# A fused convolution, scan and expert kernel: the cross-half exponents of the scan taken from rows spread by DMA and a bias of the exponential

## The chip, the core and the metric

The kernel runs on one core of one Trainium2 chip. The metric is device time in microseconds (us) of one execution, as the median of several runs. A profile is one further execution, taken by the hardware profiler, with its own time. The engines are named as the profile names them: PE does matmuls (PEld is its weight load), DVE is the vector engine, ACT the scalar engine with the activation tables, POOL the general engine, and SP issues every DMA of this kernel in one queue, in order.

## The reference, cut to what matters

The input is 128 images of 128 channels and 16 x 16 pixels, so 256 tokens per image. Layer 0 is a group norm and two quantised 3 x 3 convolutions with batch norm. Layer 1 is a state-space scan in both directions (`fwd` and `bwd`), added to the tokens, and a mixture of 8 experts of which each token takes 2. The change lies in the scan. For one direction (4 heads `h`, head width 64, state width 64) it is:

```
dt = softplus(dt + dt_bias);  A = -exp(A_log)
dA = dt * A;  xdt = xh * dt
Acs = cumsum(dA) within a chunk of 64 tokens
Y_diag = sum over s<=l of  C[l].B[s] * exp(Acs[l] - Acs[s]) * xdt[s]
states = sum over s of     B[s] * exp(Acs[last] - Acs[s]) * xdt[s]
carry  = states + carry * exp(Acs[last])          # chunk after chunk
Y_off  = C[l] . carry * exp(Acs[l])
y = (Y_diag + Y_off + xh * D) * silu(z);  RMS norm;  out_proj
```

Chunking is only a way to compute it: over the whole image, y[l] is the sum over all earlier s of C[l].B[s] * exp(cum[l] - cum[s]) * dt[s] * xh[s], with cum the running sum of dA over the 256 tokens.

## The kernel before

**The early stages.** The first 300 us or so load the images, do both convolutions and write the transposed tokens to DRAM (`y_d`). What follows is one long recorded stretch over 64 tiles `i` of two images (512 tokens) each.

**How the scan is done.** An image is cut into two halves of 128 tokens. For a tile `i`, a direction `d` and an image `k` of the tile there are three blocks of 128 source tokens (on the partitions) by 128 target tokens, for each of the 4 heads: first half to first half, first half to second half (the block between the halves), second to second. "First" is half `d`, so it is turned round for the backward direction. The exponents of one block are made by PE as one bank `sg` of 128 x 512 (4 heads x 128 targets) in `part_s`, ACT takes the exponential into `e` (tile `e0` holds the two blocks with the first half as source, `e1` the third), DVE multiplies by C.B (`g_ps`) in `part_m` (L929, L934), and PE multiplies by the tokens in `part_y` (L948, L954), which is the last reader of `e0` and `e1`. `e0` and `e1` have 4 buffers each.

**Where the exponents come from.** `part_c` works once for a group of 4 images, that is, for a pair of tiles. From dt it makes `daz` (dA) and `lwz` (minus the log of dt), and PE forms in bank `r_ps` (L784, L787, L788) three strips of 128: the running sums, the negated remaining sums with `lwz`, and `lwz` alone. DVE splits them into three bf16 parts (`part` and `left`, L794 and L797), since the exponents are rebuilt by bf16 matmuls; the parts go to DRAM (`parts_d`, L802) and come back to `rows` and `cols` (L810, L815) in the layout that `part_s` multiplies. `part_s` has three steps `j`: the two blocks within a half (two matmuls of 256 columns, L913, with a mask of -1e30 in `cols`) and the block between the halves (one matmul of 512 columns, L915).

**What sets the order.** Each `part_*` function is a stream of steps that yields between them. A table `T` written out by hand gives each step of each part its place, once for the even and once for the odd tile of a pair, and `PERIOD` is the shift from one pair to the next; all steps are sorted by place and recorded in that order. Each place is used once in a period, so that 372 places are 372 steps. Every engine works off its instructions in recorded order, and waits are put in by the framework: a buffer's next writer waits for its last reader. So a step's place fixes what stands ahead of it on its engine and, for a DMA, in SP's queue.

**Banks.** PSUM has eight banks in three groups: "x" (2) for `x_ps`, `z_ps` and `sg`, "y" (2) for `y_ps` and `f_ps`, "o" (4) for the rest. A bank of "x" comes free when ACT (for `z_ps` and `sg`) or ACT and DVE (for `x_ps`, L836 and L842) have read it.

**Other names in the text.** `part_p` loads the gates of two experts, spread over the partitions, into `gb` (L1109) and POOL multiplies the tokens into it (L1113); `part_f` multiplies by the experts (L1125) and frees `gb`. `part_o` is the output projection (L1008). `act` is the helper for all activations that need a table (its instructions stand at L675).

Of the kernel before, what the change touches and what calls it, by code (L numbers as in the profile page):

```python
# [8 lines left out]
F32 = mybir.dt.float32  # L9
# [5 lines left out]
P = 128  # L15
# [19 lines left out]
def kernel(ctx: ExitStack, tc: tile.TileContext, a: dict):  # L35
# [20 lines left out]
    parts_d = [dram.tile([2, 3, G * NH * 4, 3, P], BF16, name=f"parts_{i}", tag=f"parts_{i}") for i in range(2)]  # L56
# [558 lines left out]
    cols = [late.tile([P, 2, 2, 2, 3, P], BF16, name=f"cols{k}") for k in range(3)]  # L615
    far = late.tile([HD, 1], BF16, name="far")

    def constants():
        nc.gpsimd.memset(far, -1e30)
        none = sm.tile([NR, 3, 3 * P], BF16, name="none", tag="part", bufs=1)  # L620
        nc.gpsimd.memset(none[:, :, :P], 0.0)
        for k in range(2):
            nc.sync.dma_start(parts_d[k][1, :, :, 2, :].rearrange("q r l -> r q l"), none[:, :, :P])
        for k in range(3):
            r, c = rows[k], cols[k]
            nc.scalar.copy(r.rearrange("p h d t l -> p h (d t l)"), heads.unsqueeze(2).to_broadcast([P, NH, 4 * P]))
            nc.vector.tensor_copy(
                r[0:HD].rearrange("p h d t (f l) -> p (h d t f) l", l=HD),
                ident[0:HD, 0:HD].unsqueeze(1).to_broadcast([HD, 2 * NH * 2 * 2, HD]),
            )  # L630
            nc.vector.tensor_copy(
                c.rearrange("p m d j f l -> p m (d j f l)"), triple.unsqueeze(2).to_broadcast([P, 2, 12 * P])
            )
            for d in range(2):
                for half in range(2):
                    sign = 1 - 2 * d
                    for m in range(2):
                        nc.gpsimd.affine_select(
                            out=c[0:HD, m, d, :, half, :], in_=far.unsqueeze(2).to_broadcast([HD, 2, P]),
                            pattern=[[0, 2], [sign, P]], compare_op=ALU.is_ge, fill=0.0,  # L640
                            base=-sign * HD * half - 1, channel_multiplier=-sign,
                        )
# [10 lines left out]
    BANKS = {"x": 2, "y": 2, "o": 4}  # L653

# [11 lines left out]
    yts, uTs, xcs, xts, bcs, ccs, zs = {}, {}, {}, {}, {}, {}, {}  # L666
    table = ["none"]

    def act(out, in_, func):
# [5 lines left out]
        nc.scalar.activation(out, in_, func)  # L675
# [40 lines left out]
    def part_c(g):  # L716
# [66 lines left out]
        for d in range(2):  # L783
            nc.tensor.matmul(  # L784
                r_ps[:, : 2 * P], daz[:, d], sums[d].rearrange("p q l -> p (q l)"), start=(d == 0), stop=False
            )
        nc.tensor.matmul(r_ps[:, P : 2 * P], lwz, ident, start=False, stop=True)  # L787
        nc.tensor.matmul(r_ps[:, 2 * P : 3 * P], lwz, ident, start=True, stop=True)  # L788
        yield
        left = sm.tile([NR, 3 * P], F32, name=f"left{g}", tag="left", bufs=1)  # L790
        part = sm.tile([NR, 3, 3 * P], BF16, name=f"part{g}", tag="part", bufs=1)
        pd, rest = parts_d[g % 2], r_ps[:NR, : 3 * P]
# [8 lines left out]
        for kind, to, of, n in ((0, 1, 0, 2), (0, 0, 0, 1), (1, 0, 2, 1), (1, 1, 2, 1)):  # L801
            nc.sync.dma_start(  # L802
                pd[kind, :, :, to : to + n, :].rearrange("q r e l -> r q (e l)"), part[:, :, of * P : (of + n) * P]
            )
# [100 lines left out]
    def part_s(i, d, k, j):  # L905

        r_, c_ = rows[i % 3], cols[i % 3]
        s, t = ((d, d), (d, 1 - d), (1 - d, 1 - d))[j]
        sg = bank(f"sg{i}_{d}_{k}_{j}", "x").rearrange("p (h l) -> p h l", l=P)
        if s == t:  # L910
            for half in range(2):
                of = slice(half * HD, half * HD + HD)
                nc.tensor.matmul(sg[:, :, of], c_[:, k, d, s, half, :], r_[:, :, d, t, of], start=True, stop=True)  # L913
        else:
            nc.tensor.matmul(sg, c_[:, k, d, s, 2, :], r_[:, :, d, t, :], start=True, stop=True)  # L915
        yield
        if (i, d, k) not in es:
            es[i, d, k] = (
                pr.tile([P, NH, 2, P], F32, name=f"e0{i}_{d}_{k}", tag="e0", bufs=4),
                pr.tile([P, NH, P], F32, name=f"e1{i}_{d}_{k}", tag="e1", bufs=4),  # L920
            )
        e0, e1 = es[i, d, k]
        act(e0[:, :, t, :] if j < 2 else e1, sg, AF.Exp)
# [192 lines left out]
    def part_f(i):  # L1116
# [7 lines left out]
        for e in range(NE):  # L1124
# [10 lines left out]
    PERIOD = 372  # L1135
    T = {
        ('a',): [[221, 238, 287, 346, 471, 484], [408, 409, 420, 523, 572, 578]],
        ('c',): [
            [595, 599, 604, 612, 615, 626, 633, 649, 651, 657, 664, 680, 682, 686, 696, 706, 730, 738, 753,
             793, 802, 807, 816, 845, 883, 911, 960, 974, 1056, 1140],  # L1140
        ],
        ('x', 0, 0): [[772, 788, 790, 796, 797], [945, 951, 958, 961, 966]],
        ('x', 0, 2): [[799, 803, 811, 815, 817], [973, 983, 994, 996, 999]],
        ('x', 0, 1): [[829, 835, 848, 849, 857], [1012, 1026, 1033, 1042, 1044]],
        ('x', 1, 2): [[871, 876, 882, 888, 892], [1048, 1057, 1063, 1064, 1070]],
        ('x', 1, 0): [[881, 890, 893, 897, 898], [1072, 1080, 1092, 1093, 1094]],
        ('x', 1, 1): [[925, 930, 932, 936, 942], [1114, 1121, 1131, 1135, 1137]],
        ('z', 1, 0): [[943, 949], [1148, 1150]],
        ('bc',): [[962, 990], [1143, 1166]],
        ('sx', 0): [[975], [1178]],  # L1150
        ('z', 0, 0): [[956, 964], [1158, 1163]],
        ('sx', 1): [[988], [1161]],
        ('z', 1, 1): [[972, 979], [1132, 1138]],
        ('z', 0, 1): [[992, 997], [1180, 1186]],
        ('g', 0): [[1003], [1191]],
        ('s', 0, 0, 0): [[1007, 1015], [1192, 1193]],
        ('xt', 0, 0): [[1038, 1046], [1204, 1232]],
        ('s', 0, 1, 0): [[1000, 1010], [1198, 1200]],
        ('s', 0, 0, 1): [[1016, 1027], [1206, 1212]],
        ('s', 0, 0, 2): [[1034, 1037], [1216, 1226]],  # L1160
        ('m', 0, 0): [[1047, 1055], [1233, 1237]],
        ('xt', 1, 0): [[1017, 1041], [1195, 1199]],
        ('s', 0, 1, 1): [[1043, 1053], [1239, 1241]],
        ('s', 1, 1, 0): [[1060, 1062], [1246, 1250]],
        ('s', 0, 1, 2): [[1082, 1086], [1273, 1275]],
        ('xt', 0, 1): [[1051, 1081], [1245, 1256]],
        ('s', 1, 0, 2): [[1108, 1116], [1285, 1287]],
        ('g', 1): [[1099], [1282]],
        ('m', 0, 1): [[1115, 1119], [1290, 1291]],
        ('s', 1, 0, 0): [[1096, 1103], [1266, 1268]],  # L1170
        ('s', 1, 1, 1): [[1088, 1100], [1292, 1293]],
        ('xt', 1, 1): [[1107, 1120], [1294, 1296]],
        ('s', 1, 0, 1): [[1104, 1109], [1274, 1286]],
        ('m', 1, 1): [[1129, 1134], [1313, 1324]],
        ('s', 1, 1, 2): [[1117, 1123], [1301, 1309]],
        ('y', 0, 1): [[1126, 1149, 1156, 1167], [1311, 1320, 1327, 1407]],
        ('y', 0, 0): [[1130, 1146, 1147, 1172], [1310, 1319, 1326, 1342]],
        ('m', 1, 0): [[1141, 1145], [1300, 1329]],
        ('y', 1, 1): [[1155, 1170, 1218, 1223], [1340, 1352, 1386, 1394]],
        ('y', 1, 0): [[1190, 1214, 1224, 1225], [1365, 1376, 1391, 1402]],  # L1180
        ('n', 0): [[1230], [1431]],
        ('n', 1): [[1231], [1412]],
        ('r',): [[1249, 1251, 1257, 1261, 1272], [1437, 1443, 1447, 1448, 1461]],
        ('o', 0): [[1259, 1281], [1451, 1467]],
        ('o', 1): [[1271, 1284], [1456, 1473]],
        ('e',): [
            [1288, 1303, 1312, 1325, 1335, 1341, 1350, 1353, 1357, 1361, 1367, 1373, 1374, 1378, 1381, 1383,
             1397, 1404, 1417, 1421, 1422, 1433, 1439, 1441, 1446, 1449, 1455, 1457, 1459, 1469, 1477],
            [1485, 1490, 1499, 1511, 1514, 1526, 1529, 1531, 1545, 1548, 1549, 1553, 1557, 1566, 1574, 1575,
             1577, 1581, 1582, 1583, 1585, 1594, 1599, 1606, 1608, 1612, 1614, 1616, 1630, 1635, 1650],  # L1190
        ],
        ('p', 0): [[1484, 1505, 1508], [1667, 1678, 1690]],
        ('p', 1): [[1500, 1569, 1591], [1703, 1735, 1757]],
        ('f',): [
            [1554, 1568, 1580, 1607, 1610, 1624, 1651, 1661, 1671, 1677, 1679],
            [1721, 1752, 1764, 1768, 1783, 1810, 1835, 1855, 1866, 1868, 1895],
        ],
        ('p', 2): [[1556, 1619, 1648], [1730, 1762, 1817]],
        ('p', 3): [[1649, 1652, 1670], [1772, 1842, 1850]],
# [3 lines left out]
        "s": part_s, "m": part_m, "y": part_y, "n": part_n, "r": part_r, "o": part_o, "e": part_e, "p": part_p,  # L1203
# [44 lines left out]
```

## Time and profile before

| | |
|---|---|
| median of 3 runs | 2648.76 us (2643.7 to 2649.42) |
| profiled execution: time, span | 2651.35 us, 2649.6 us |
| mean granted PE clock | 0.984 |
| PE busy, share of the span | 2499.6 us, 94% |
| DVE | 2416.2 us, 91% |
| ACT | 2030.1 us, 77% |
| POOL | 1654.9 us, 62% |
| mean busy share of the DMA engines, 660 to 2340 us | 0.29 |
| DMA traffic in the same window | 91 GB/s |

The span runs from the first instruction to the last; the profiled execution's own time is 1.75 us longer. Busy time counts an instruction from its start to its modelled end, so two matmuls that overlap in PE's pipeline are counted once together, but one alone is shown longer than the slot it takes. A share over the whole span is a mean over the early stages, the recorded stretch in its steady part (from about 400 to 2590 us) and the ends.

### The profile page before, as it was taken

Reading aid. Unit: us, or ns where it says so; the run is one execution under the profiler, and the core shown is the slowest. Engines: PE = TensorE matmul, PEld = TensorE weight load, DVE = VectorE, ACT = ScalarE, POOL = GpSimd, SP = SyncE. Lnnn points to the kernel's source line nnn. Section 1 sums busy time; section 2 is a strip of 40 time slices with the busy share of each in tenths; the row PEclk is TensorE's granted clock in tenths of the full one; section 3 lists DMA queues with packets and bytes.
Section 4 is the critical chain, followed back from the end, with each engine's and each line's share of the span. In section 5 each row is a group of like instructions: output and inputs, shape, how many; then the busy total and the mean of one; then the engine's idle time right before and its main releaser. Section 6 shows DMA issues by size and latency. Waiting matters only on the chain.

```text
span 2649.6 us, 47721 instructions
## 1 busy us (share of the span) xinstructions
PE 2499.6 (94%) x16004; PEld 1493.9 (56%) x16004; DVE 2416.2 (91%) x6161; ACT 2030.1 (77%) x3682; POOL 1654.9 (62%) x1728
## 2 busy tenths in 40 slices
PE   0889589999999999999999999999999999999997
PEld 0335345666666656666666666666666666666663
DVE  8877589999999999999999999999999999999984
ACT  6877478878877888787778887877788878777771
POOL 1886314666666666666666666666666666666666
PEclk9999789999999999999999999999999999999998
DMA  8468311323222233232223332332223323322223
GB/s 276 152 213 284 122 27 56 96 91 98 91 93 84 86 97 97 89 98 91 84 87 90 94 98 90 98 95 89 86 84 98 97 89 98 97 85 82 86 89 104
DMA packets 165705, 275.58 MB, mean 104 GB/s; under 512 B 46528, under 2 KB 89536, under 8 KB 165440
## 3 DMA queue, kind: packets, MB, share of 16 engines
q1 hardware_dynamic: 165440, 272.32, 32.7%
q8 instruction: 132, 2.16, 0.3%
q14 instruction: 133, 1.09, 0.1%
HBM read 197.45 MB, written 58.03 MB: 96 GB/s over the span
## 4 chain that ended last, share of the span: by engine, by line
PE 84%; DVE 7%; POOL 3%; ACT 2%; issue 2%; DMA 1%; SPq 0%; POOLq 0%; DVEq 0%; ACTq 0%
PE f_ps L1125 16%; PE x_ps L824 12%; PE o_ps L1008 9%; PE y_ps L948 8%; PE z_ps L867 8%; PE sg L913 4%; PE xt_ps L879 4%; PE y_ps L954 4%; PE g_ps L898 4%; PE cv L221 4%; PE sg L915 2%; POOL xr L591 1%; PE n_ps L981 1%; DVE bc L842 1%; PE u_ps L710 1%
## 5 line engine op out<-in xcount | busy, mean ns | idle before, releaser
L1113 POOL TENSOR_TENSOR gb<-gb,u2T 128x512 f32<-128x512 f32 x512 | 646.5, 1279 | 130.5 <-DMA gb<-gd 112.6
L842 DVE SCALAR_TENSOR_TENSOR xc<-x_ps,cw,xc 128x510 f32<-128x510 f32 (+2 forms) x768 | 572.4, 745 | 54.4 <-ACT xc L836 39.5
L675 ACT ACTIVATE e<-sg 128x512 f32<-128x512 f32 x768 | 451.0, 592 | 207.1 <-PE sg L913 168.2
L1125 PE MATMUL f_ps<-gb,ew 128*128 128x512 f32 x1024 | 525.9, 607 | 5.5 <-POOL gb L1113 5.1
L964 POOL TENSOR_TENSOR yg<-yg,z 128x512 f32<-128x512 f32 x256 | 323.7, 1275 | 276.3 <-DVE yg L960 276.2
L824 PE MATMUL x_ps<-uT,wx 128*128 128x512 f32 x768 | 401.7, 605 | 7.1 <-DVE bc L842 2.8
L948 PE MATMUL y_ps<-e,xt 128*64 128x256 f32 x2048 | 317.7, 389 | 0.3 <-DVE yg L960 0.2
L836 ACT ACTIVATE xc<-x_ps,cb,cw 128x512 f32<-128x512 f32 x256 | 199.5, 779 | 147.1 <-PE x_ps L824 145.1
L929 DVE TENSOR_TENSOR e<-e,g_ps 128x1024 f32<-128x1024 f32 x256 | 310.1, 1212 | 2.2 <-PE g_ps L898 2.2
L842 DVE SCALAR_TENSOR_TENSOR bc<-x_ps,cw,bc 128x510 f32<-128x510 f32 (+2 forms) x384 | 283.6, 738 | 4.4 <-ACT bc L836 2.0
L867 PE MATMUL z_ps<-uT,wz 128*128 128x512 f32 x512 | 276.7, 622 | 1.2 <-DVE xc L842 0.8
L1008 PE MATMUL o_ps<-wo,yg 128*128 128x128 f32 x2048 | 250.8, 276 | 0.0
L1008 PEld LDWEIGHTS o_ps<-wo,yg 128*128 128x128 f32 x2048 | 240.1, 193 | 10.6 <-DVE g L1087 8.7
L1125 PEld LDWEIGHTS f_ps<-gb,ew 128*128 128x128 f32 x1024 | 171.1, 192 | 82.2 <-issue 52.0
L913 PE MATMUL sg<-rows,cols 128*128 128x256 bf16 x1024 | 197.1, 274 | 9.0 <-DVE sel L1068 4.0
L954 PE MATMUL y_ps<-e,xt 128*64 128x128 f32 x2048 | 198.9, 273 | 0.9 <-DVE e L934 0.9
L824 PEld LDWEIGHTS x_ps<-uT,wx 128*128 128x128 f32 x768 | 131.9, 193 | 118.1 <-issue 59.4
L221 PE MATMUL cv<-hpad,wq 128*128 128x512 bf16 x640 | 180.5, 426 | 16.7 <-DVE hpad L194 8.6
L996 POOL TENSOR_TENSOR rr<-rr,mhalf 128x8 f32<-128x8 f32 x64 | 105.4, 1647 | 142.8 <-DVE rr L992 142.8
L960 DVE SCALAR_TENSOR_TENSOR yg<-xc,dcol,y_ps 128x512 f32<-128x512 f32 x256 | 184.4, 741 | 8.0 <-PE y_ps L954 8.0
L954 PEld LDWEIGHTS y_ps<-e,xt 128*64 128x64 f32 x2048 | 147.0, 137 | 75.1 <-DVE e L934 1.3
L675 ACT ACTIVATE z<-z_ps 128x512 f32<-128x512 f32 x256 | 152.1, 594 | 42.6 <-PE z_ps L867 35.2
(255 smaller groups left out, 4947.3 us busy)
## 6 DMA issues: line engine op xcount, KB each, us to landing
gb<-gd SPq DMA_DIRECT2D x256, 512.0 KB
xr<-in_x SPq DMA_DIRECT2D x64, 256.0 KB
y<-yt SPq DMA_DIRECT2D x64, 256.0 KB
yt<-y SPq DMA_DIRECT2D x64, 256.0 KB
cc<-bc SPq DMA_DIRECT2D x128, 128.0 KB
out<-ob SPq DMA_DIRECT2D x64, 256.0 KB
o<-o SPq DMA_DIRECT2D x59, 256.0 KB
q<-o SPq DMA_DIRECT2D x59, 256.0 KB
```

What stands on the lines that cost most here:

```text
L675: nc.scalar.activation(out, in_, func)
L824: nc.tensor.matmul(ps, wx[d][:, n * P : (n + 1) * P], uTs[i], start=True, stop=True)
L842: nc.vector.scalar_tensor_tensor(acc[:, :, to], raw[:, :, of], cw[:, d, n, 3 - back : 4 - back], acc[:, :, to], ALU.mult, ALU.add,)
L867: nc.tensor.matmul(ps, wz[:, d, n * P : (n + 1) * P], uTs[i], start=True, stop=True)
L913: nc.tensor.matmul(sg[:, :, of], c_[:, k, d, s, half, :], r_[:, :, d, t, of], start=True, stop=True)
L929: nc.vector.tensor_tensor(e0.rearrange("p h t l -> p h (t l)"), e0.rearrange("p h t l -> p h (t l)"), gps[i, d, k][:, 0:NT].unsqueeze(1).t ...
L948: nc.tensor.matmul(y_ps[64 * q : 64 * q + 64, k, :], xt[:, 2 * k + s0, 64 * h : 64 * h + 64], e0[:, h].rearrange("p t l -> p (t l)"), star ...
L954: nc.tensor.matmul(y_ps[64 * q : 64 * q + 64, k, s1 * P : (s1 + 1) * P], xt[:, 2 * k + s1, 64 * h : 64 * h + 64], e1[:, h, :], start=False ...
L964: nc.gpsimd.tensor_tensor(yg, yg, zs[i, d][:, n, :], ALU.mult)
L1008: nc.tensor.matmul(o_ps[:, (2 * j + d) * P : (2 * j + d + 1) * P], ygs[i, d, n][:, t * P : (t + 1) * P], wo[d][:, n, :], start=(n == 0), s ...
L1113: nc.gpsimd.tensor_tensor(gb[:, e], gb[:, e], u2Ts[i], ALU.mult)
L1125: nc.tensor.matmul(f_ps, ew[:, e, :], gbs[i, e], start=False, stop=(e == NE - 1))
```

## The change

The block between the halves needs exp(cum[l] + end[s]), where cum[l] is the target's running sum from the border of the halves and end[s] the source's remaining sum with the log of dt: a row for each head and a column for each head. Its matmul goes. A new part `b` has the row of each of the 4 heads spread by DMA over all 128 partitions, straight into the block's place in `e0`, and ACT then takes the exponential in place, one instruction for each head, with the column `ends` as its bias. `part_c` makes the rows (`cum`, copied by ACT and written to DRAM as `cum_d`) and the columns (`ends`, by four narrow matmuls and a DVE instruction). The strips that are split in bf16 parts are two instead of three, `cols` and its DMAs shrink by a third, `e0` gets a fifth buffer, and all places in `T` are new, with 375 steps in a period.

```diff
-    parts_d = [dram.tile([2, 3, G * NH * 4, 3, P], BF16, ...) for i in range(2)]
+    parts_d = [dram.tile([2, 3, G * NH * 4, 2, P], BF16, ...) for i in range(2)]
+    cum_d = [dram.tile([G * NH * 4, P], F32, ...) for i in range(2)]
...
-    cols = [late.tile([P, 2, 2, 2, 3, P], BF16, name=f"cols{k}") for k in range(3)]
+    cols = [late.tile([P, 2, 2, 2, 2, P], BF16, name=f"cols{k}") for k in range(3)]
...
-        none = sm.tile([NR, 3, 3 * P], BF16, name="none", tag="part", bufs=1)
-        nc.gpsimd.memset(none[:, :, :P], 0.0)
-        for k in range(2):
-            nc.sync.dma_start(parts_d[k][1, :, :, 2, :]..., none[:, :, :P])
...
+    E0 = 5
...
         r_ps = bank(f"r_ps{g}", "o")
         for d in range(2):
-            nc.tensor.matmul(
-                r_ps[:, : 2 * P], daz[:, d], sums[d].rearrange("p q l -> p (q l)"), start=(d == 0), stop=False
-            )
-        nc.tensor.matmul(r_ps[:, P : 2 * P], lwz, ident, start=False, stop=True)
-        nc.tensor.matmul(r_ps[:, 2 * P : 3 * P], lwz, ident, start=True, stop=True)
-        yield
-        left = sm.tile([NR, 3 * P], F32, name=f"left{g}", tag="left", bufs=1)
-        part = sm.tile([NR, 3, 3 * P], BF16, name=f"part{g}", tag="part", bufs=1)
+            nc.tensor.matmul(r_ps[:, :P], daz[:, d], sums[d][:, 0, :], start=(d == 0), stop=(d == 1))
+        nc.tensor.matmul(r_ps[:, P : 2 * P], lwz, ident, start=True, stop=True)
+        own = lambda t, d: t.rearrange("p (r d j) -> p r d j", d=2, j=2)[:, :, d, d]
+        for d in range(2):
+            at = slice(2 * P + d * G * NH, 2 * P + (d + 1) * G * NH)
+            nc.tensor.matmul(r_ps[:, at], sums[d][:, 1, :], own(daz[:, d, :NR], d), start=True, stop=False)
+            nc.tensor.matmul(r_ps[:, at], ident, own(lwz[:, :NR], d), start=False, stop=True)
+        yield
+        cum = sm.tile([NR, P], F32, name=f"cum{g}", tag="cum", bufs=1)
+        nc.scalar.copy(cum, r_ps[:NR, :P])
+        yield
+        ends = ends_[g] = sm.tile([P, 2, G, NH], F32, name=f"ends{g}", tag="ends")
+        nc.vector.tensor_scalar(ends..., r_ps[:, 2 * P : 2 * P + 2 * G * NH], -1.0, None, ALU.mult)
+        yield
+        nc.sync.dma_start(cum_d[g % 2], cum)
+        yield
+        left = sm.tile([NR, 2 * P], F32, name=f"left{g}", tag="left", bufs=1)
+        part = sm.tile([NR, 3, 2 * P], BF16, name=f"part{g}", tag="part", bufs=1)
...
     def part_s(i, d, k, j):
-        s, t = ((d, d), (d, 1 - d), (1 - d, 1 - d))[j]
+        s = (d, 1 - d)[j]
...
-            nc.tensor.matmul(sg, c_[:, k, d, s, 2, :], r_[:, :, d, t, :], start=True, stop=True)
...
+    def part_b(i, d, k):
+        e0, t, m = blocks_of(i, d, k)[0], 1 - d, 2 * (i % 2) + k
+        of = cum_d[i // 2 % 2].rearrange("(m h d j) l -> m h d j l", m=G, h=NH, d=2)[m, :, d, t, :]
+        nc.sync.dma_start(e0[:, :, t, :], of.partition_broadcast(P))
+        yield
+        for h in range(NH):
+            act(e0[:, h, t, :], e0[:, h, t, :], AF.Exp, bias=ends_[i // 2][:, d, m, h : h + 1])
+        yield
...
-    PERIOD = 372
+    PERIOD = 375
     T = {
-        ('a',): [[221, 238, 287, 346, 471, 484], [408, 409, 420, 523, 572, 578]],
+        ('a',): [[291, 329, 430, 443, 610, 624], [515, 532, 570, 614, 677, 681]],
...
+        ('b', 0, 0): [[973, 1152], [1269, 1302]],
+        ('b', 0, 1): [[1103, 1202], [1094, 1346]],
...
+        ('b', 1, 1): [[1150, 1172], [1315, 1367]],
+        ('b', 1, 0): [[1151, 1217], [1322, 1384]],
...
-        ('y', 1, 1): [[1155, 1170, 1218, 1223], [1340, 1352, 1386, 1394]],
+        ('y', 1, 1): [[1271, 1285, 1318, 1332], [1442, 1451, 1477, 1498]],
...
-        ('p', 0): [[1484, 1505, 1508], [1667, 1678, 1690]],
+        ('p', 0): [[1611, 1612, 1636], [1785, 1836, 1838]],
...
-            [1721, 1752, 1764, 1768, 1783, 1810, 1835, 1855, 1866, 1868, 1895],
+            [1855, 1860, 1868, 1883, 1906, 1913, 1962, 1972, 1978, 1979, 2031],
```

In `T`, the first list is the even tile's places and the second the odd tile's; of a part `b` the first place is the DMA, the second the four exponentials. The last two lines shown are the odd tile's part `f`, the last of all.

## The prediction

> **What bounds the kernel now.** I read the page's busy shares and slices first. After the early stages PE and DVE are both full, so the mean shares do not say which of them sets the pace.
>
> ```profile
> PE 2499.6 (94%) x16004; PEld 1493.9 (56%) x16004; DVE 2416.2 (91%) x6161; ACT 2030.1 (77%) x3682; POOL 1654.9 (62%) x1728
> ...
> PE   0889589999999999999999999999999999999997
> ...
> DVE  8877589999999999999999999999999999999984
> ```
>
> Then the busy time of a steady window, 660 to 2340 us. A pair of tiles takes 16 multiplies of L1113, and the groups of 1000 to 2400 us have 317 of them: 19.8 pairs in 1400 us, so 70.7 us a pair. Per pair the window below gives PE 70.6, DVE 67.9 (96.1%), ACT 56.6 (80%), POOL 46.2 us.
>
> ```profile
> 660.00:2340.00 1680.00, 1676.66 (x11215) 1032.10 (x11214) 1614.27 (x4174) 1345.69 (x2427) 1097.99 (x1046) 1.00 0.29 91
> ```
>
> A busy PE may still be waiting under its modelled ends, so I went to PE's timeline for the starts.
>
> ```profile
> 1505.17 1.03 PE L784 MATMUL r_ps<-sums,daz 128*128 128x256 f32 x4
> 1506.04 0.38 PE L787 MATMUL r_ps<-ident,lwz 128*128 128x128 f32 x2
> 1506.26 0.39 PE L788 MATMUL r_ps<-ident,lwz 128*128 128x128 f32 x2
> 1506.48 1.02 PE L824 MATMUL x_ps<-uT,wx 128*128 128x512 f32 x2
> ...
> 1517.53 0.38 PE L915 MATMUL sg<-rows,cols 128*128 128x512 bf16 x1
> 1517.75 1.07 PE L824 MATMUL x_ps<-uT,wx 128*128 128x512 f32 x2
> ```
>
> The next start follows L915 after 0.22 us, though it is shown as 0.38 long; two of L787 take 0.22. The same kinds take the same slots all along the timeline. PE waits for nearly nothing, and its work is a sum of slots. The waits agree: DVE waits for ACT, ACT for PE, POOL for DVE.
>
> ```profile
> POOL yg L964 <- DVE yg L960: 181.5, 93, 3.5
> ...
> ACT xc L836 <- PE x_ps L824: 109.0, 167, 1.6
> ...
> DVE xc L842 <- ACT xc L836: 24.8, 80, 0.5
> ```
>
> So PE sets the pace, and DVE is only 2.8 us a pair behind it.
>
> A rule speaks against this reading. The Trainium skill (Perfetto Trace Analysis, Identifying the Most-Contended Engine) holds matmul busy time to be a poor measure and asks for weight-load time on PE and occupancy on DVE; that is 61% (1032.10 of 1680) against 96%. By the rule DVE is the bound, and only what DVE saves would count, some 0.35 us a pair. I go by the starts; the engine's own order of slots is direct.
>
> **The change, part by part (per pair; PE counted by slots).**
>
> *PE, removed.* 8 of L915 (256 over 32 pairs) at 0.215: -1.72 us. Two "x" banks are asked for 8 times less.
>
> *PE, `r_ps`.* Before: 1505.17 to 1506.48, 1.31 us. After: half of L784's 0.87 (the strip of 128 columns) is 0.44, one L787 0.22, and four narrow matmuls of 16 columns, two rows each as for every fp32 one here. The trace has no matmul so narrow. From below, streaming by columns gives 16/128 of 0.11, together 0.11 us for 8 rows. From above, the shown weight load of a 128 x 128 fp32 row (190 ns in r_ps) gives 1.52. I take the slot of a 128-wide row, 0.11, since o_ps (L1008) loads new weights for each such row and still fits it: 0.88. Sum 1.54, so +0.23 (-0.54 to +0.87). The skill's page TensorE: Matmul & The Clock Gate (Back-to-back issue gap) names a floor of about 25 ns for a narrow matmul; by that the eight cost 0.2 and PE saves 0.7 more. No run here shows it.
>
> PE in all: -1.49 us (-0.85 to -2.26).
>
> *ACT.* Removed: 8 exponentials of 0.59, which take 0.49 each where they follow each other (see below, four in 1.65 instead of 4 x 0.49). Added: 32 of 128 x 128 with one bias column, SBUF to SBUF.
>
> ```profile
> L987 ACT ACTIVATE ns<-n_ps 128x128 f32<-128x128 f32 x64 | 17.7, 277 | 3.3 <-PE n_ps L981 3.2
> L696 ACT ACTIVATE u<-t,nmrb,rstdb 128x128 f32<-128x128 f32 x256 | 105.5, 492 | 0.8 <-POOL nmrb L693 0.8
> L518 ACT ACTIVATE o<-cv,less 128x512 f32<-128x512 f32 x59 | 40.1, 683 | 6.0 <-PE cv L221 2.7 <-DMA o<-o 1.2
> ...
> 1532.68 1.65 ACT L696 ACTIVATE u<-t,nmrb,rstdb 128x128 f32<-128x128 f32 x4
> ```
>
> Bounds: 0.28 (no column, from PSUM) and 0.49 (two columns). One column costs about 0.09 (L518 at 0.683 beside 0.59), SBUF instead of PSUM 0.03 (L967 at 0.626 beside 0.59): 0.39 each, 0.29 back to back, four in 1.26. So 8 x 1.26 - 8 x 0.49 + 0.24 for the `cum` copy = +6.4 us; the upper bound (8 x 1.65) gives +9.5. ACT goes from 56.6 to 63 (66), of 69 to 70: 91% (95%). The cost is hidden by ACT's idle 14 us, of which some 6 remain. Table loads do not change, 4 a pair.
>
> *DVE.* The splitting (L794 0.54 + 2 x 0.34, L797 0.54 + 0.54) is 2.3 us on 384 columns. L842 against L1018 (0.745 for 510 columns, 0.342 for 128) gives 1.05 ns a column, so 128 fewer save 0.13 on each of three, and half on the two bf16 casts: -0.54. `ends` costs +0.19 (L1058, 128x32). -0.35 (0 to -0.6).
>
> *SP and DMA.* 34 issues a pair become 43: 8 of `b` and the `cum` write, at 0.3 to 0.75 us each (rows of the queue), +3 to +7 us, beside long idle stretches. Data: 8 x 256 KB on 6.4 MB (91 GB/s), so the busy share goes from 0.29 to about 0.39. Hidden.
>
> *The new waits.* A `b` DMA waits on SP until `part_y` has read one of the five `e0` buffers for the last time, and for `cum`; behind it in SP's queue stand the `cc` halves, the `parts` writes and the next `gb`, for which PE and POOL wait. Its four exponentials wait on ACT for the landing; behind them stand the readers of the "x" banks, and PE behind those. The places between DMA and exponential are 22 in the tightest case (`b` 1,1 of the even tile) and 33 to 252 in the others; at 69.2 us for 375 places, 22 are 4.1 us. What a landing takes:
>
> ```profile
> 1561.37 0.68 SPq L1103 DMA_DIRECT2D gd<-gT  x1
> 1563.38 0.80 SPq L1109 DMA_DIRECT2D gb<-gd  x2
> ...
> 1567.61 2.51 POOL L1113 TENSOR_TENSOR gb<-gb,u2T 128x512 f32<-128x512 f32 x2 [2.41 <-DMA gb<-gd]
> ```
>
> 16 KB were there after 2.0 us (the next issue waited for them), the first of two reads of 512 KB after 4.2; for 256 KB I take the middle, 3.1 (2.0 to 4.2). So it lands in time unless SP is late. Cost nothing; without that cover see the last rival.
>
> `p` 0 of the even tile now has its multiply one place after its DMA (21 before), so POOL stands some 4 us there. POOL has 24 us idle a pair; behind it wait `part_y`'s multiplies. Nothing, at worst included in the friction below.
>
> *The ends.* First place to last is 1674 of 372 before (4.50 periods), 1740 of 375 after (4.64). Outside 32 x 70.7 us and the first 304 us the span has 83 us for 3.5 periods of depth, 24 a period: +3.3. Ahead of the stretch three DVE copies of `cols` (1.74 each) shrink by a third, of which the last is on the path: -0.6, and a POOL memset goes: about -0.6.
>
> **The sum.** PE is full for some 31 pairs (400 to 2590 us). With PE 1.49 us shorter, DVE would be busy 67.55 of 69.2, 97.6%. Stretches at 400 and 500 us show DVE at 19.72 of 20, so that is possible, but never over a whole steady window. If DVE kept its 96.1%, the pair would take 70.3 and 1.1 of the gain be lost; I take a third of that as friction, 0.35, since it is shown to run closer. So -1.14 x 31 = -35.3, +3.3 - 1.2: -33 us. The profiled execution of 2651.35 becomes 2618; it stands 2.6 above the median, so 2615 for the median. Own range: friction 0 to 0.8 and PE -0.85 to -1.9 give 2590 to 2640.
>
> **Rivals.**
>
> *All of it arrives.* The narrow matmuls cost little and DVE packs as tightly as in the short stretches: -1.5 to -2.1 a pair, 2583 to 2602. For: PE's gapless starts. Against: three engines over 90%.
>
> *DVE becomes the bound.* At its 96.1% the pair takes 67.55/0.961 = 70.3: -0.4 x 31 + 2 = -10, 2638. For: 2.8 us between the two now. Against: its named waits end at PE.
>
> *Slower: reads that land after their turn on ACT.* SP is one queue, and it stands still at `gb` issues that wait for PE:
>
> ```profile
> SPq L1109 <- PE f_ps L1125: 431.9, 46, 11.2
> ```
>
> That is 9.4 us each time in 1400 us. A `b` read behind such a stop, or behind the wait for an `e0`, starts late; its exponentials stop ACT, which has 6 us of idle left, and with both "x" banks unread PE stops. Two late reads a pair of 2 us each, less the 0.9 that the other bank covers, are 2.2; less 1.5 saved, +0.7 a pair: 2648.8 + 22 + 2 = 2673. It decides from about 1.5 us lost on PE a pair, a read 3 us late at one place or 2.4 at two. Against: seven of eight have 6 us or more. At one more us it is 2700.
>
> **Chances.** Forecast 0.38, all of it 0.13, DVE 0.17, late reads 0.32. A measurement here tells 0.2%, 5.3 us, from no change. Faster: the forecast but for 0.01, all of it, and 0.09 of DVE: 0.59. Same: 0.01 + 0.08 of DVE: 0.09. Slower 0.32. The range leaves out a tenth at each end: the best of the full saving, and late reads beyond 2690.
>
> **What would show it.** Right: no L915 in the page and PE's steady window still full; L784's bank at about 1.5 us of slots; the new exponentials at 0.39 and ACT near 91%; DVE over 97%; 69 to 70 us a pair. Wrong: waits of ACT for the DMA of `cum` to `e`, PE below 98% with ACT as its releaser, SP waits before `e` followed by late `gb`, exponentials at 0.5.

## The result, and the profile after

The changed kernel takes 2666.55 us (median of four runs, 2665.32 to 2668.08) against 2649.09 for the kernel before: the ratio is 1.007, 95% interval 1.0052 to 1.0087. It is slower by 17.5 us where the prediction said 34 us faster.

The pair of tiles gives the difference at once. ACT's copy `ns` runs once a tile; in the window 660 to 2400 us its first and last start, 48 copies apart, give 70.57 us a pair before (673.4 to 2367.2) and 71.45 after (670.3 to 2385.1). The prediction had 69.43. All pairs below are measured so, over as many whole pairs as fit.

The page of the changed kernel: busy shares, slices, and the chain that ended last.

```profile
PE 2461.6 (92%) x15940; PEld 1471.0 (55%) x15940; DVE 2393.3 (90%) x6193; ACT 2206.7 (83%) x4482; POOL 1661.8 (62%) x1727
...
PE   0889689999999999999999999999999999999997
...
PE 65%; DVE 26%; POOL 3%; ACT 2%; issue 2%; DMA 1%; SPq 0%; POOLq 0%; DVEq 0%; ACTq 0%
```

The slices still show a full PE. The chain does not: DVE holds 26% of it, where it held 7% in the kernel before:

```profile
PE 84%; DVE 7%; POOL 3%; ACT 2%; issue 2%; DMA 1%; SPq 0%; POOLq 0%; DVEq 0%; ACTq 0%
```

Busy time of the steady window (length; PE, PEld, DVE, ACT, POOL; clock, DMA share, GB/s):

```profile
660.00:2340.00 1680.00, 1632.72 (x11034) 1001.61 (x11032) 1581.55 (x4134) 1459.14 (x2984) 1089.57 (x1034) 1.00 0.41 119
```

Of its 1680 us PE is busy 1632.72, where it was 1676.66. With 23.5 pairs in the window that is 2 us a pair in which PE stands still. The waits of the same window name them:

```profile
PE sg L923 <- DVE xc L853: 47.3, 47, 1.3
...
DVE ends L794 <- ACT cum L791: 28.8, 23, 1.3
DVE lg L1080 <- PE rt_ps L1066: 15.0, 23, 0.7
```

In the kernel before PE had one named wait in this window, and a small one:

```profile
PE sg L913 <- DVE sel L1068: 3.3, 10, 0.4
```

Now, twice a pair and for 1.0 us in the mean, PE waits at a matmul `sg` for DVE's convolution product `xc`, the last reader of an `x_ps` in an "x" bank that `sg` needs. DVE itself waits 1.25 us a pair at `ends`, a step that the change brought, behind ACT's `cum` copy.

The chain in the second of the two places (start, length, what): PE hands over to DVE at 1552.83 and takes the chain back at 1561.64.

```profile
1552.57 0.24 PE y_ps L976 x4
1552.83 0.75 DVE yg L982
1553.58 0.65 DVE bc L853
1554.23 0.75 DVE w L748
1555.34 0.20 DVE sel L1087
1556.01 0.20 DVE sel L1094
1556.89 1.29 DVE sel L1087
1558.55 0.46 DVE w L760
1559.06 0.65 DVE xc L853
1559.71 0.37 DVE sel L1094
1560.15 0.67 DVE xc L853
1560.84 0.76 DVE xc L853
1561.64 0.38 PE sg L923 x2
```

Between PE's hand-over and the three products of `xc` stand steps of the router (`sel`) and of the softplus (`w`). One `sel` of 128 x 32 takes 1.29 us, more than six times the 0.20 of the same line a moment earlier. The timeline says what was beside it:

```profile
1556.69 0.77 ACT L847 ACTIVATE xc<-x_ps,cb,cw 128x512 f32<-128x512 f32 x1
1556.87 1.26 POOL L995 TENSOR_TENSOR sq<-sq,sq 128x512 f32<-128x512 f32 x1 [1.94 <-ACT sq L989]
1556.89 1.29 DVE L1087 TENSOR_TENSOR sel<-lg,mx 128x32 f32<-128x32 f32 x1
```

It started just behind a POOL instruction and ended with it, at 1558.2. ACT had finished its part of `xc` at 1557.46; the products could have run then. The other place has the same pattern twice: L1097 from 1521.14 to 1522.39 beside a POOL multiply that ends at 1522.36, and L1087 from 1523.19 to 1524.41 beside a POOL addition that ends at 1524.36.

### The profile page after: what moved, and what is told of

It is laid out like the page before. It is cut to its first block, busy times and chain, and to the rows that moved or that the text cites. A ratio compares the mean times of both kernels' runs of the same rounds, so it can differ in the third digit from the quotient of the medians.

```text
span 2663.6 us, 49217 instructions
## 1 busy us (share of the span) xinstructions
PE 2461.6 (92%) x15940; PEld 1471.0 (55%) x15940; DVE 2393.3 (90%) x6193; ACT 2206.7 (83%) x4482; POOL 1661.8 (62%) x1727
## 4 chain that ended last, share of the span: by engine, by line
PE 65%; DVE 26%; POOL 3%; ACT 2%; issue 2%; DMA 1%; SPq 0%; POOLq 0%; DVEq 0%; ACTq 0%
PE z_ps L878 9%; PE f_ps L1147 9%; PE o_ps L1030 8%; PE x_ps L835 8%; PE y_ps L970 8%; DVE xc L853 5%; PE y_ps L976 4%; PE cv L222 3%; DVE bc L853 3%; DVE sel L1087 3%; PE sg L923 3%; PE xt_ps L890 2%; PE g_ps L909 2%; DVE yg L982 2%; DVE lg L1097 2%
## 5 line engine op out<-in xcount | busy, mean ns | idle before, releaser
L1135 POOL TENSOR_TENSOR gb<-gb,u2T 128x512 f32<-128x512 f32 x512 | 641.8, 1280 | 11.2 <-DMA gb<-gd 11.1
L853 DVE SCALAR_TENSOR_TENSOR xc<-x_ps,cw,xc 128x510 f32<-128x510 f32 (+2 forms) x768 | 570.4, 743 | 24.8 <-ACT xc L847 12.7
L986 POOL TENSOR_TENSOR yg<-yg,z 128x512 f32<-128x512 f32 x256 | 332.6, 1302 | 368.9 <-DVE yg L982 348.1
L1147 PE MATMUL f_ps<-gb,ew 128*128 128x512 f32 x1024 | 535.3, 607 | 2.9 <-POOL gb L1135 2.8
L673 ACT ACTIVATE e<-sg 128x512 f32<-128x512 f32 x512 | 296.9, 593 | 143.3 <-PE sg L923 132.9
L673 ACT ACTIVATE e<-e,ends 128x128 f32<-128x128 f32 x1024 | 325.4, 393 | 0.0
L853 DVE SCALAR_TENSOR_TENSOR bc<-x_ps,cw,bc 128x510 f32<-128x510 f32 (+2 forms) x384 | 284.5, 741 | 17.2 <-ACT bc L847 14.8
L923 PE MATMUL sg<-rows,cols 128*128 128x256 bf16 x1024 | 186.5, 274 | 68.4 <-DVE xc L853 62.5
L995 POOL TENSOR_TENSOR sq<-sq,sq 128x512 f32<-128x512 f32 x128 | 162.8, 1273 | 108.9 <-ACT sq L989 108.2
L673 ACT ACTIVATE z<-z_ps 128x512 f32<-128x512 f32 x256 | 152.8, 597 | 69.6 <-POOL gb L1135 32.9
L982 DVE SCALAR_TENSOR_TENSOR yg<-xc,dcol,y_ps 128x512 f32<-128x512 f32 x256 | 189.8, 741 | 19.7 <-PE y_ps L976 19.7
L923 PEld LDWEIGHTS <-cols 128*128 128x128 bf16 x1024 | 89.6, 98 | 207.2 <-issue 190.7
```

The costliest lines, as they stand in the source:

```text
L673: nc.scalar.activation(out, in_, func, **more)
L853: nc.vector.scalar_tensor_tensor(acc[:, :, to], raw[:, :, of], cw[:, d, n, 3 - back : 4 - back], acc[:, :, to], ALU.mult, ALU.add,)
L986: nc.gpsimd.tensor_tensor(yg, yg, zs[i, d][:, n, :], ALU.mult)
L1135: nc.gpsimd.tensor_tensor(gb[:, e], gb[:, e], u2Ts[i], ALU.mult)
L1147: nc.tensor.matmul(f_ps, ew[:, e, :], gbs[i, e], start=False, stop=(e == NE - 1))
```

## The experiments

Each ratio is to the kernel before as it ran in the same round (medians of 2646 to 2649 us), with its 95% interval.

| kernel | us | ratio | pair, us |
|---|---|---|---|
| before | 2649.09 | 1 | 70.57 |
| changed | 2666.55 | 1.007 [1.0052, 1.0087] | 71.45 |
| `ends_late` | 2659.12 | 1.0046 [1.003, 1.0063] | 71.12 |
| `old_plan` | 2689.47 | 1.0159 [1.0139, 1.0179] | 72.13 |
| `new_plan_matmul` | 2792.97 | 1.0553 [1.0536, 1.0571] | 75.38 |
| `before_less_dve` | 2645.0 | 0.9989 [0.998, 0.9999] | 70.52 |
| `no_reads` | 2664.59 | 1.0077 [1.0057, 1.0097] | 71.45 |
| `one_exp` | 2668.95 | 1.0081 [1.006, 1.0103] | 71.44 |
| `after_less_pe` | 2645.36 | 1.0 [0.9989, 1.0012] | 70.87 |
| `after_less_dve` | 2663.08 | 1.0068 [1.005, 1.0086] | 71.44 |
| `sg_later` | 2656.72 | 1.0028 [1.0017, 1.0039] | 71.04 |
| `conv_first` | 2611.43 | 0.9855 [0.9836, 0.9874] | 69.64 |
| `all_three` | 2611.12 | 0.9854 [0.9833, 0.9875] | 69.66 |
| `all_four` | 2656.94 | 1.0028 [1.0018, 1.0038] | 71.04 |
| `first_stretch` | 2619.49 | 0.9893 [0.9877, 0.991] | 69.96 |
| `second_stretch` | 2655.23 | 1.0032 [1.0022, 1.0041] | 71.12 |
| `no_sq_sum` | 2603.97 | 0.9838 [0.9821, 0.9854] | 69.6 |

### Does one engine pace the kernel?

`before_less_dve` and `after_less_dve` make the same cut in both kernels:

```diff
-        nc.vector.tensor_tensor(
-            e1, e1, gps[i, d, k]... , ALU.mult
-        )
+        if k == 1:
+            nc.vector.tensor_tensor(e1, e1, gps[i, d, k]... , ALU.mult)
```

> The kernel before, leaving out half of the 128 x 512 products with `g` (four of eight a pair, 0.68 us each on DVE, 2.7 us a pair); every other engine does the same work. If PE's slots set the pace of the kernel before, as the prediction took it: within 0.3% of 2649. If DVE sets it: up to 2.7 us a pair less until PE's 70.6 is all that is left, so between; a fall of over 10 us says that some of PE's 70.6 was waiting for DVE.

> The changed kernel, leaving out half of the 128 x 512 products with `g` (2.7 us a pair on DVE), the same cut that moved the kernel before by only 0.1%. If PE alone sets the pace: again within 5 us, 2661 to 2670. Theory A: PE's 2.3 us a pair of waiting for DVE's `xc` shrinks by what of the cut lies in those two stretches, 2620 to 2655. If DVE alone: 31 x 2.7 = 84 us less until PE binds, near 2600.

Neither moved its pair (70.57 to 70.52, and 71.45 to 71.44). DVE's total is the bound of neither kernel: leaving out four products of 0.68 us a pair (DVE's busy time fell by 2.3 and 2.2 us a pair) buys at most 0.05. The expectation of theory A for the second was a miss: the cut products lie outside the two stretches, and PE's wait stays what it was.

```profile
PE sg L923 <- DVE xc L853: 47.0, 47, 1.3
```

`after_less_pe` takes from PE:

```diff
-                    e0[:, h].rearrange("p t l -> p (t l)"), start=True, stop=False,
+                    e0[:, h].rearrange("p t l -> p (t l)"), start=True, stop=(k == 0),
...
-            for q in range(2):
+            for q in range(2 * k):
```

> The changed kernel, leaving out half of `part_y`'s second matmuls (those of e1 for k = 0): some 0.22 us of PE's slots for each of the eight steps, 1.8 us a pair. If PE alone sets the pace of the changed kernel, as the prediction had it: 31 x 1.8 = 55 us less, near 2611. Theory A (the chain passes from PE to DVE and back twice a pair): only PE's part of it shrinks, 2625 to 2655. If DVE alone: within 5 us of 2666.

The mean pair fell by 0.58 of 1.8 us. But part of that is the clock: in each of the ten runs of this kernel the granted PE clock was 0.976 to 0.980, in those of the changed kernel 0.984 or 0.985. The profile shows the clock halved for 3.4 us in some pairs, for instance at 952.0 us. Three pairs without such a stretch and two with one in each:

```profile
1381.00:1591.00 210.00, 202.60 (x1311) 122.33 (x1309) 202.17 (x528) 184.99 (x381) 138.82 (x132) 1.00 0.42 121
1095.00:1239.00 144.00, 139.08 (x875) 83.35 (x876) 135.40 (x354) 123.95 (x256) 92.50 (x88) 0.98 0.40 118
```

The first three last 70.17 us each, the other two 71.85. Why this kernel's clock fell is not shown. At the full clock, then, 1.28 of the 1.8 us arrived, and the waits at `sg` grew by the rest, 0.5 us a pair (59.1 us in the window where there were 47.3). So where PE has the chain it sets the pace, and a part of what it saves ahead of those two places it loses there.

### ACT, the reads, the order

`no_reads` replaces the input of the small exponentials by a constant tile; `one_exp` merges the four.

```diff
-        nc.sync.dma_start(e0[:, :, t, :], of.partition_broadcast(P))
...
-            act(e0[:, h, t, :], e0[:, h, t, :], AF.Exp, bias=ends_[i // 2][:, d, m, h : h + 1])
+            act(e0[:, h, t, :], still[:, h, :], AF.Exp, bias=ends_[i // 2][:, d, m, h : h + 1])
```

> The changed kernel without the eight spread reads a pair: the small exponentials take their input from one constant SBUF tile instead. ACT, DVE, PE and POOL do the same work; SP has 8 issues a pair fewer and the DMA share falls from 0.41 to about 0.3. Left out: the data of the blocks between the halves. Theory A (PE and DVE wait for each other in the new order; DMA is no part of it): 2660 to 2672, as the changed kernel's 2666. Theory B (the reads cost, through SP or through traffic): 2620 to 2650.

```diff
-        for h in range(NH):
-            act(e0[:, h, t, :], e0[:, h, t, :], AF.Exp, bias=...)
+        act(e0[:, :, t, :], e0[:, :, t, :], AF.Exp)
```

> The changed kernel with one exponential of 128 x 512 without a bias for each block instead of four of 128 x 128 with one: ACT loses 8 x (1.26 - 0.6) = 5.3 us a pair. Left out: the bias. Theory A (PE and DVE wait for each other): 2655 to 2668, since no wait of either but the 1.25 us at `ends` ends at ACT. Theory C (ACT's load is what the change costs): 2620 to 2645.

Neither changed the pair. The busy time of the steady window, `no_reads` first:

```profile
660.00:2340.00 1680.00, 1632.76 (x11034) 1001.66 (x11032) 1580.78 (x4135) 1459.24 (x2983) 1089.84 (x1033) 1.00 0.29 89
```

```profile
660.00:2340.00 1680.00, 1633.01 (x11034) 1001.54 (x11034) 1580.35 (x4135) 1353.27 (x2419) 1090.33 (x1035) 1.00 0.41 119
```

The DMA share fell from 0.41 to 0.29 in the one, ACT's busy time by 106 us in the other; PE's and DVE's columns stayed within 1.2 us. Neither the traffic of the reads, nor their eight issues on SP, nor the 32 small exponentials cost anything in this order of steps.

`old_plan` runs the new mechanism at the old places, with `ends` behind the first subtraction; the reads and `cum` needed places of my choice. `new_plan_matmul` runs the old matmul at the new places.

```diff
-    PERIOD = 375
+    PERIOD = 372
...
+        ('b', 0, 0): [[945.5, 1027], [1110.5, 1212]],
+        ('b', 0, 1): [[955.5, 1053], [1145.5, 1241]],
+        ('b', 1, 1): [[1000.5, 1100], [1175.5, 1293]],
+        ('b', 1, 0): [[1005.5, 1109], [1200.5, 1286]],
```

> The new mechanism in the order of before: the places and the period (372) of the kernel before, the exponentials of the spread rows at the places of the exponentials they replace, their reads 60 to 120 places earlier, `cum` and `ends` put between the old places (`ends` behind the first subtraction). Theory 1 (DVE's stop at `ends` is the loss): that stop is not here, so DVE's 67.5 us busy and before's 2.7 us idle make 70.2 a pair, 2630 to 2642 us. Theory 2 (the new order is the cost, the mechanism is a gain): 2605 to 2630, PE's shorter work shows. Theory 3 (the small exponentials and the traffic cost): 2655 to 2690, in whatever order.

> The kernel before, with its matmul for the blocks between the halves, in the new order: the places and the period (375) of the changed kernel, the matmul and its exponential near the place of the four small exponentials (up to 40 places earlier where the two banks ask for it); no `cum`, no `ends`. Theory 1: no stop at `ends`, DVE busy 67.9 and idle 2.7 as before: 2645 to 2660. Theory 2 (the new order costs about 0.9 + 1.5 us a pair by itself): 2680 to 2730. Theory 3: like the kernel before, 2645 to 2655.

Both mixtures are slower than both kernels, so these two runs do not price plan and mechanism apart. `new_plan_matmul` lies beyond all three of its ranges; it also has only the four `e0` buffers of the kernel before in an order made for five. `old_plan` lies in theory 3's range, but not for theory 3's reason, since neither the exponentials nor the traffic cost anything in the other order. In `old_plan` some transfers come late for DVE and PE, and SP stands at the reads until an `e0` is free:

```profile
SPq L943 <- PE y_ps L971: 103.8, 86, 2.3
...
DVE s6a L683 <- DMA yt<-y: 34.8, 46, 2.9
...
PE g_ps L910 <- DMA cc<-bc: 10.2, 14, 1.4
```

Late transfers are what the prediction's slower rival feared, though these are others than it named. That the reads make them late is not shown: in the changed kernel SP stands longer at the reads, 168.2 us in the window, and neither PE nor DVE waits for a transfer. Nor are they all of the 72.13: PE also waits 21.0 us for DVE's `xc` there.

### DVE's stop at `ends`

```diff
         nc.scalar.copy(cum, r_ps[:NR, :P])
         yield
-        ends = ends_[g] = sm.tile(...)
-        nc.vector.tensor_scalar(ends..., r_ps[...], -1.0, None, ALU.mult)
-        yield
...
                 rest = left
                 yield
+                if q == 0:
+                    ends = ends_[g] = sm.tile(...)
+                    nc.vector.tensor_scalar(ends..., r_ps[...], -1.0, None, ALU.mult)
+                    yield
```

> The changed kernel with DVE's `ends` product one step group later: after the first subtraction of the splitting (place 921.5) instead of straight behind ACT's `cum` copy (place 904). Nothing else is touched. Theory 1 (DVE paces the changed kernel, and its new stop of 1.25 us a pair at `ends` is what was lost): the stop goes, some 31 x 1.25 = 39 us less at most, 2627 to 2640 us against 2666, PE's waits at `sg` shrink from 2.3 us a pair towards 1. Theory 2 (the new order of steps as a whole is the cost, many small waits): only a part comes back, 2655 to 2666. Theory 3 (ACT's 32 small exponentials or the DMA traffic of the spread rows set the pace): no change, 2663 to 2669.

The stop went, and 0.33 us a pair with it, of 1.25. DVE then waited longer for `lg` (24.1 us in the window instead of 15.0), and PE's wait at `sg` only fell to 40.0. The time, 2659.12 us, is in theory 2's range. Theory 1 was wrong in size: a stop of DVE counts by what of it reaches the products that PE waits for.

### The order of DVE at the two places

`conv_first` moves the three products of `x` (0, 1) together, ahead of the router's next steps, in both tiles. No instruction is added or removed.

```diff
-        ('x', 0, 1): [[938, 942, 950, 967, 968], [1115, 1134, 1139, 1146, 1149]],
+        ('x', 0, 1): [[938, 942, 950, 950.2, 950.4], [1115, 1128.05, 1128.1, 1128.2, 1128.3]],
...
-            [..., 1687, 1698, 1699, 1701, ...]     # ('e',), odd tile
+            [..., 1687, 1700.5, 1700.6, 1701, ...]
```

> The changed kernel with the convolution products of `x` (0, 1) put on DVE right behind one another and ahead of the next router and softplus steps, in both tiles (places 950, 950.2, 950.4 and 1128.1 to 1128.3; ACT's step of the odd tile at 1128.05, the router's update of `lg` and its maximum behind them). These products read a PSUM bank for which PE waits at `sg` (2.3 us a pair); in the changed kernel small router steps that last as long as POOL's instruction beside them stand between the products. Theory A (PE sets the pace, and loses what it waits there for DVE's order): DVE frees the bank about 1 to 3 us earlier, PE's waits at `sg` go, up to 31 x 2.0 = 62 us: 2605 to 2640. Theory D (DVE's total work sets the pace; it is only reordered here): 2660 to 2670. Theory E (the wait moves on to the router's chain, which is now later: `gd`, `gb`, POOL, `f_ps`): 2650 to 2675 with new waits of PE at `f_ps`.

It takes 1.81 us off the pair and beats both kernels: 2611.43 us, 1.45% under the kernel before. The steady window and what is left of PE's named waits:

```profile
660.00:2340.00 1680.00, 1671.65 (x11314) 1028.14 (x11314) 1591.17 (x4247) 1501.87 (x3069) 1116.13 (x1060) 1.00 0.42 121
```

```profile
PE sg L923 <- DVE bc L853: 8.3, 24, 0.6
```

47.3 us of waiting became 8.3 (0.35 a pair), and DVE still stops at `ends` (25.3 us in the window) without harm. `first_stretch` and `second_stretch` make the move in one tile alone.

> conv_first in one place alone: the products of the even tile (950, 950.2, 950.4, the router's steps behind them). If each place has its own price: about 1.1 us of the 1.81 us a pair, 2628 to 2638. If PE only waits at the other place instead: 2655 to 2667.

> conv_first in the other place alone: the products of the odd tile (1128.1 to 1128.3). If each place has its own price: about 0.7 us a pair, 2638 to 2648. If PE only waits at the other place instead: 2655 to 2667.

The even tile's place is worth 1.49 us a pair, the odd tile's 0.33; together 1.82 against 1.81 measured, so each has its own price. Both sizes were missed, the first put at 1.1 and the second at 0.7. PE's waits in the changed kernel were 1.34 us in the first place (at 1526.71) and 0.66 in the second (at 1561.64). The second returned only half because PE then waits there for the product that follows, of `bc`; with `second_stretch` the window has

```profile
PE sg L923 <- DVE xc L853: 32.1, 24, 1.3
PE sg L923 <- DVE bc L853: 7.5, 23, 0.3
```

the first place's old wait and 0.33 us at the second. Why the first returned a little more than its wait is not known.

`all_three` adds the later `ends` and a later `lg` (1677.5 for 1663 in the odd tile); `sg_later` leaves DVE as in the changed kernel and puts the waiting `sg` behind the next matmuls of PE; `all_four` has everything.

> conv_first together with `ends` behind the first subtraction (ends_late) and the copy `lg` of the odd tile behind the `bc` products (1677.5 for 1663), where DVE waited 0.65 us for PE's `rt_ps`. Theory A: PE is nearly gapless, 69.1 to 69.8 us a pair, 2600 to 2625, which is the forecast for the change as written. Theory D: DVE's idle falls by 1.9 us, 2610 to 2640. Theory E: 2645 to 2665.

```diff
-        ('s', 1, 1, 0): [[1158, 1165], [1350, 1352]],
+        ('s', 1, 1, 0): [[1163.5, 1165], [1354.5, 1356.5]],
```

> The changed kernel with the `sg` that waits, `s` (1, 1, 0), moved on PE's side instead: behind the next matmuls of `r` and `f` (1163.5 for 1158, 1354.5 for 1350), so that PE has 1.4 us of other work while DVE frees the bank. DVE's order is untouched. Theory A: most of PE's 2 us a pair go, 2610 to 2645. Theory D: 2660 to 2670. Theory E: the wait is passed to the next user of the banks, `x` (1, 0), and on: 2650 to 2668.

> all_three and sg_later together. Theory A: as all_three or a few us less, 2598 to 2622. Theory D: as all_three. Theory E: as all_three or slower, since the exponentials behind `sg` come later.

`all_three` equals `conv_first` (69.66): without its stops at `ends` and `lg` DVE is only busy for longer, and mostly by steps that take longer (`rstda` of L686, a step on four columns, has a mean of 0.83 us there and 0.24 in `conv_first`: 40.0 us in the window against 11.5).

```profile
660.00:2340.00 1680.00, 1671.24 (x11314) 1030.16 (x11312) 1629.61 (x4248) 1500.39 (x3068) 1117.14 (x1061) 1.00 0.42 121
```

`sg_later` gains 0.41 us a pair and no more. PE no longer waits for DVE; it waits at the next user of the bank, for the exponential that reads `sg`:

```profile
PE x_ps L835 <- ACT e L673: 33.0, 48, 0.7
```

`all_four`, where DVE is no longer late, has the same pair (71.04) and the same wait:

```profile
PE x_ps L836 <- ACT e L673: 33.0, 48, 0.7
```

So this wait is not DVE's lateness handed on: the later `sg` makes it by itself, and in `all_four` it costs 1.38 us a pair. Theory A was a miss for both; theory E's range held for `sg_later`. With two banks a matmul put off takes its reader with it.

### What holds the small steps

`no_sq_sum` leaves DVE's order as the changed kernel has it and takes away a POOL instruction:

```diff
         sq = sqs[i, d, 0]
-        nc.gpsimd.tensor_tensor(sq, sq, sqs[i, d, 1], ALU.add)
         yield
```

> The changed kernel, leaving out POOL's two additions of the squares a tile (`part_n`); DVE's order and work are untouched. In the second of the two stretches before `sg` the router step L1087 lasted 1.29 us where 0.19 is its least, and ended with that addition. If DVE's step is held by POOL's instruction: its long cases fall to 0.2 there, DVE frees the bank about 1 us earlier, the wait at `sg` of the second stretch goes, 0.7 to 1 us a pair, 2635 to 2648. If the long steps have another cause (or another POOL instruction moves into the place): the steps stay at 1.2 us, and the time at 2660 to 2668.

The pair falls to 69.6, further than expected, because the addition had held DVE in both places. The step `sel`, its shortest, median and longest duration in ns over the steady window, is L1087 in the changed kernel and L1086 here:

```profile
L1087 DVE TENSOR_TENSOR sel<-lg,mx x94: 191/704/1303, 662.1 to 2309.1; 128x32 f32<-128x32 f32 x94
```

```profile
L1086 DVE TENSOR_TENSOR sel<-lg,mx x96: 180/192/195, 687.1 to 2326.1; 128x32 f32<-128x32 f32 x96
```

Not one is long any more. In the changed kernel 47 of the 94 took over 0.3 us, and each of these ended with the addition, L995, which had begun before it. PE's wait at `sg` is 7.2 us in the window. That POOL's instruction held DVE's is shown by this. That all of the 1.85 us a pair comes through DVE is likely and not shown, since POOL also loses 5 us of work a pair.

## Why the prediction was wrong, point by point

**What bounds the kernel: right.** PE paces the kernel before; four products a pair less on DVE moved it by 0.1%. The rule weighed against this (the Trainium skill, Perfetto Trace Analysis, Identifying the Most-Contended Engine), by which DVE at 96% would have been the bound, is not borne out by either kernel.

**PE's sum: nearly right.** The steady chain after prices `r_ps` at 1508.95 to 1510.42, 1.47 us against 1.54 predicted:

```profile
1508.95 0.45 PE r_ps L782 x4
1509.40 0.22 PE r_ps L783 x2
1509.75 0.22 PE r_ps L788 x2
1509.98 0.22 PE r_ps L787 x2
1510.20 0.22 PE r_ps L788 x2
1510.42 0.95 PE z_ps L878 x2
```

Two rows of a narrow matmul take 0.22 us, the slot of 128 columns, as the prediction took it. The floor of about 25 ns that the Trainium skill's page TensorE: Matmul & The Clock Gate (Back-to-back issue gap) names for a narrow matmul is not reached; each row here loads new weights, but that this is the reason is not shown. `conv_first` runs at 69.64, or 69.3 less what is left of its wait, where the sum without friction said 69.1. So some 0.2 of the 1.49 us did not come.

**ACT: right.** The new exponentials take 0.39 us, four of them 1.26, ACT's sum of 62.1 us a pair (1459.14 over 23.5) was put at 63, and hiding it was right (`one_exp`).

```profile
L673 ACT ACTIVATE e<-e,ends 128x128 f32<-128x128 f32 x752 | 238.9, 392 | 0.0
```

The last column is the idle time before them: they never waited for a read. So the rival of late reads, at 0.32 the only one on the slower side, had the sign and not the mechanism: SP did wait before `e` (168.2 us in the window), but no `gb` was late for it.

**DVE's total: right, and beside the point.** 1581.55 over 23.5 pairs is 67.3 us, predicted 67.55.

**The ends: wrong, and hidden.** They were put at +2.1 us (3.3 less 1.2). The changed kernel loses 31 times 0.88, that is 27 us, in its pairs and 17.5 in all, so by this estimate the ends are about 10 us shorter; in `conv_first` they are 9. Part of it stands at the start: the first copy `ns` is at 386.2 us in the changed kernel and at 394.4 before. What shortens them was not followed. That `conv_first` takes 2611 us, close to the predicted 2615, is therefore partly luck: its pair is 0.2 us longer than the forecast 69.43, and its ends are shorter.

**The friction: the step that failed.** It was put at 0.35 us a pair, a third of what DVE would lose if it kept its share of busy time. What came was about 2.4, the pair of 71.45 less the sum's 69.1. Of it 2.0 are PE's two waits at `sg`; the other 0.4 lie under PE's busy time, and `conv_first` still has some 0.2 of them. The friction was worked out from DVE's total, and a total says nothing of it. What counts is which step of DVE PE waits for, and what the new plan put in front of that step: the products of the even tile moved from places 848, 849 and 857 to 950, 967 and 968, with five router steps and one of the splitting between the first and the second. The prediction followed the moved DMAs and a moved POOL step past their queues, and no moved DVE step. Its view of the banks (two "x" banks asked for 8 times less) counted requests, not how late the last reader comes.

The row that should have warned was in the trace of before. A 128 x 32 step of the router had a mean of 675 ns; its shortest, median and longest in the steady window were

```profile
L1075 DVE SCALAR_TENSOR_TENSOR lg<-sel,lg x48: 191/674/1167, 665.2 to 2323.9; 128x32 f32<-128x32 f32 x48
```

and the 24 long ones each ended with a POOL instruction that had begun earlier. Some of DVE's steps that read two SBUF operands last until POOL's instruction ends. The Trainium skill has a rule for this (SBUF — State Buffer, Who interferes with whom): a VectorE instruction with two SBUF inputs (against a GpSimd instruction that reads SBUF), or a copy, cast or `tensor_scalar` in a two-port mode, shares a port pair with GpSimd, and whoever comes second is blocked for the whole instruction; one SBUF input outside those modes, or a reduction, is not. The changed kernel's trace agrees in the lines looked at: L853, one of whose two operands is in PSUM, never takes over 750 ns, the reduction L1085 never over 189; L1087 reaches 1303 from a least of 191, and the cast L804 from SBUF 834 from a least of 277. By the rule the convolution products are the steps to run while POOL is busy, and the router's are not to stand ahead of them.

**The new waits.** `ends` behind `cum` was not in the prediction; it is 1.25 us of DVE a pair, worth 0.33 in this plan and nothing in `conv_first`. The p 0 multiply, taken to cost POOL about 4 us of standing, did not: POOL's wait for `gb` reads nearly vanished (11.1 us in the whole run; 80.1 in the steady window alone before).

## What to carry to other kernels

Where one engine is full and the next is 3 us behind it, price a new order by the steps that the full engine waits for: take each bank that it shares, find the last reader, and count what the new plan puts ahead of that reader, at the duration that those steps have beside POOL. A total of busy time, right to 0.3 us as it was here, doesn't say whether it fits. When a plan is made anew, move the reader rather than the writer: putting the matmul later made the bank's next user wait for it.

## What the runs showed of the hardware

- A DVE step of 0.19 us with both operands in SBUF lasted up to 1.30 us, to the end of the POOL instruction that had started before it (47 of 94 times); without that POOL instruction none on this line took over 195 ns.
- DVE's busy share counts such holding: `all_three` and `conv_first` take the same time, with DVE busy 1629.61 and 1591.17 us of the same 1680. A DVE at 97% was not a DVE that set the pace.
- An fp32 matmul of 16 columns with new weights took the same 0.11 us a row as one of 128.
- The granted PE clock can differ between kernels that differ little: `after_less_pe` showed 0.976 to 0.980 in ten runs, the changed kernel 0.984 or 0.985 in four; a stretch of 3.4 us at half the clock went with a pair longer by 1.7 us.
